# Attention masks of a two-layer graph network: 32x32 squares on VectorE, rows in blocks of 32, and left sides kept in SBUF

## The chip, the cores and the metric

The kernel runs on one core of one Trainium2 chip. The metric is the device time of one execution in microseconds (us). The median over six runs stands for the kernel, and one execution was recorded by the hardware profiler.

## The reference

There are N = 2708 nodes with D = 1024 features, all in fp32, and one integer adjacency matrix `adj` of 2708 x 2708. Both layers normalize, attend over the neighbours and add the result to their input. Biases and vectors are left out here where they change nothing in the shape of the work.

```
h  = relu(layernorm(x))
f  = h @ Wf + bf ;  g = h @ Wg + bg
e  = relu(f @ g.T)
x  = x + softmax(where(adj > 0, e, NEG)) @ (h @ W + bW)

h  = relu(layernorm(x)) @ W1
e  = leaky_relu(h @ a1 + (h @ a2).T, 0.2)
x  = x + relu(softmax(where(adj > 0, e, NEG)) @ h)
```

The mask of `adj` enters both layers. In the first layer it is added to the scores `e`; in the second it comes back from a copy in DRAM.

## The kernel before

**Tiling.** The 2708 rows are cut into five panels: `width` is 576, 576, 532, 512 and 512 rows, and `base` holds their starts. Each panel has F = 4 full tiles of 128 rows. The 64, 64 and 20 rows that are left over in the first three panels form two more tiles, `MONO` and `TINY`. `start_of_tile` (L95) and `places` (L97) say which rows of the input belong to which partitions of a tile; in this kernel a full tile is 128 rows in sequence. The twenty full tiles go in ten `pairs`, numbered q = 0 to 9, and the two left-over tiles are one more unit, `LEFT`. Nearly every large matrix product is made by a Strassen-Winograd scheme with seven half-sized products, M1 to M7.

**Stages of layer 0.** Wf and Wg are first multiplied into one matrix. Then each panel p goes through five steps. One multiplies the panel's rows by that matrix, `scores(p)` makes the scores against all rows, a softmax follows, one step aggregates, and `project` multiplies by W and adds the residual. The scores lie transposed: the panel's 512 to 576 rows run along the free axis, and the other nodes lie on the partitions. So the mask needs `adj` transposed as well. Layer 1 comes after the five panels.

**The loop of `scores(p)` (L1030).** For each pair q it forms seven products in the order M1, (M4 of the pair before), M6, M5, M2, M7, M3. `product` (L1043) loads the left sides `As` from `hs_d` in DRAM, two products at a time, and issues eight or four matmuls (L1052). VectorE takes each product out of PSUM with an addition; all VectorE instructions are issued through one helper, so they have line 45. `finish` then adds the mask, keeps the running maximum in `acc`, and, where layer 1's vectors are known, also updates the maximum for layer 1. While `nc.hold` is set, VectorE's instructions stay in program order. DMAs from SP go through `load` (L136) and always stay in program order; stores go from POOL (L140).

**The mask (`mask_maker`, L651).** `fetch(q)` loads a block of `adj` with SP, two pairs ahead. `convert(q)` turns it into 0 or minus BIG in bf16 (`nm`, and `nmt` for the 64 or 20 rows beyond 512). `turn(q)` transposes `nm` on TensorE in 128x128 blocks into a PSUM bank `mk_ps` (L700, tail L705), ScalarE copies the bank to `mask` (L701, L706), and POOL stores it to `mk_d` for layer 1. In the loop, `convert(q + 1)` stands behind M5's eviction and `turn(q + 1)` behind M3's. The first unit's three steps are done in the stages before (`first_masks`).

**Pairs in the background (`make_pairs`, L320).** Panel 0 finds its left sides being made as it goes. For each pair: x is loaded by SP, VectorE and ScalarE normalize, POOL forms sums for the aggregation (`pair_h`, L297), TensorE transposes (`h_ps`, L340), ScalarE copies to four tiles `hsT`, VectorE makes four sums in them, and POOL stores them to `hs_d`. `dots` form a bias per row. These steps are queued with `put`, each with an estimated cost, and `behind(rate)` takes some of them after each product, as much as a credit allows; `make_until(q)` forces the queue until pair q is made. In `scores` the two are called as

```
        rate = (0.6, 1.0, 0.65, 0.65, 0.65)[p]
            make_until(q + 2)
```

**Pools.** `slots` has 54 buffers, `strm` 12 (x blocks, `hsT`, `As`, `adj_i`, `g1` and `g2` share it) and `psum` 8 banks.

Of the kernel before, what the change touches and what calls it, by code (L numbers as in the profile page):

```python
# [10 lines left out]
I32 = mybir.dt.int32  # L11
# [46 lines left out]
def kernel(  # L58
# [22 lines left out]
    NH = NC // 2  # L81


    NP = N // W
    NM = P // 2
    NY = N - NP * W - P
# [5 lines left out]
    NT = TINY + 1  # L92
    full = lambda p: range(F * p, F * (p + 1))
    panel_of = [p for p in range(NP) for _ in range(F)] + [1, 2]
    start_of_tile = lambda t: base[t // F] + t % F * P  # L95

    places = [[(slice(0, P), start_of_tile(t))] for t in range(MONO)]  # L97
    places.append([(slice(0, NM), base[0] + W), (slice(NM, P), base[1] + W)])
    places.append([(slice(B32 * g, B32 * g + NY), base[2] + W) for g in range(P // B32)])

# [62 lines left out]

    ident = consts.tile([P, P], FP, name="ident")
    make_identity(nc, ident)
    identb = consts.tile([P, P], BF, name="identb")
    nc.vector.tensor_copy(identb, ident)
# [17 lines left out]
    def put(us, go, fetch=None, takes_psum=False, ready=None):  # L185
        later.append([us, fetch, go, takes_psum, ready])
# [128 lines left out]
    c0 = consts.tile([P, 1], FP, name="c0")  # L315
    r_ = consts.tile([P, NCOL], FP, name="r")
    vb = [None, None]
    made, turned_tiles = set(), set()

    def make_pairs():  # L320
        xs, hT = {}, {}
# [39 lines left out]
        def sums(q):  # L361
            if q == LEFT:
                return
            ts, i = hT.pop(q)
            at = {m: i(k) for k, m in enumerate(BY_SCORES)}
            add(at[M5], i(7), at[M4])
            sub(at[M6], at[M5], at[M1])
            sub(at[M7], at[M1], i(7))
            sub(at[M3], at[M2], at[M6])
            for g, t in enumerate(ts):  # L370
                store(hs_d[q][:, 2 * g:2 * g + 2].rearrange("p m c j -> p (m c j)"), t.rearrange("p m c j -> p (m c j)"))
# [28 lines left out]
        for i, q in enumerate(todo):  # L400
            if i + 1 < len(todo):
                put_norms(todo[i + 1])
            put_rows(q)
            put(0.5, lambda q=q: transposes(q), takes_psum=True)
            if i > 1:
                put_dots(q)
            put(2.7 if q != LEFT else 0.0, lambda q=q: last(q))
            if i == 1:
                put_dots(todo[0])
                put_dots(todo[1])  # L410
# [240 lines left out]
    def mask_maker(p):  # L651

        r0, w = base[p], width[p]
        k4 = w // P
        tail = w - k4 * P
        raw, neg = {}, {}

        def fetch(q):
            a = stream("adj_i", (P, k4, 2, P), I32)
            b = slot("adj_t", (P, 2, P), I32) if tail else None  # L660
            raw[q] = a, b
            body = adj[r0:r0 + k4 * P].rearrange("(i p) j -> p i j", p=P)
            last = adj[r0 + k4 * P:r0 + w]
            if q < LEFT:
                j0 = start_of_tile(pairs[q][0])
                load(a.rearrange("p i k j -> p i (k j)"), body[:, :, j0:j0 + 2 * P])
                if tail:
                    load(b[:tail].rearrange("p k j -> p (k j)"), last[:, j0:j0 + 2 * P])
                return
            for k, at, j, n in ((0, 0, base[0] + W, NM), (0, NM, base[1] + W, NM), (1, 0, base[2] + W, NY)):  # L670
                load(a[:, :, k, at:at + n], body[:, :, j:j + n])
                if tail:
                    load(b[:tail, k, at:at + n], last[:, j:j + n])

        def negate(o, i):
            nc.vector.tensor_scalar(o, i, 0.0, -BIG, op0=OP.is_le, op1=OP.mult)

        def convert(q):
            a, b = raw.pop(q)
            m = [slot("nm", (P, k4, 2, P), BF)]  # L680
            if tail:
                m.append(slot("nmt", (P, 1, 2, P), BF))
            for n, o, i in [(P, m[0], a)] + ([(tail, m[1], b.rearrange("p (o k) j -> p o k j", o=1))] if tail else []):
                if q < LEFT:
                    negate(o[:n], i[:n])
                    continue
                r = o.shape[1]
                nc.gpsimd.memset(o[:, :, 1], -BIG)
                negate(o[:n, :, 0], i[:n, :, 0])
                negate(o[:n, :, 1].rearrange("p i (g c) -> p i g c", c=B32)[:, :, :, :NY],  # L690
                       i[:n, :, 1:2, :NY].to_broadcast([n, r, P // B32, NY]))
            neg[q] = m

        def turn(q):
            m = neg.pop(q)
            mk = slot("mask", (P, 2, WX), BF)
            ps = bank("mk_ps", (P, 2, W), BF)
            for k in range(2):
                for i in range(k4):
                    nc.tensor.transpose(ps[:, k, i * P:(i + 1) * P], m[0][:, i, k], identb)  # L700
            nc.scalar.copy(mk[:, :, :k4 * P], ps[:, :, :k4 * P])  # L701
            if tail:
                ps = bank("mk_ps", (P, 2, W), BF)
                for k in range(2):
                    nc.tensor.transpose(ps[:, k, :tail], m[1][:tail, 0, k], identb[:tail, :tail])  # L705
                nc.scalar.copy(mk[:, :, k4 * P:w], ps[:, :, :tail])  # L706
            store(mk_d[p][:, q], mk[:, :, :w])
            mk_sb[p, q] = mk

        return fetch, convert, turn  # L710

# [2 lines left out]
    def first_masks(p, step):  # L714
        fetch, convert, turn = makers[p]
        if step == 0:
            fetch(0)
            fetch(1)
        elif step == 1:
            convert(0)  # L720
        else:
            turn(0)

    def load_mask(p, q, k):
        mt = slot("maskl", (P, WX), BF)
# [304 lines left out]
    def scores(p, B):  # L1030
# [6 lines left out]
        spread(rb, columns_of(p, r_[:, first_col[p]:]))  # L1037
        acc = slot("acc")
        S = [None] * NT
        rate = (0.6, 1.0, 0.65, 0.65, 0.65)[p]  # L1040
        lefts = {}

        def product(q, m, ps, start):  # L1043
            n, i = P, BY_SCORES.index(m)
            if i % 2 == 0:
                t = stream("As", (P, 2, NH, P))
                lefts[q] = t
                k = min(2, 7 - i)
                load(t[:, :k].rearrange("p m c j -> p (m c j)"),
                     hs_d[q][:, i:i + k].rearrange("p m c j -> p (m c j)"))  # L1050
            for c in range(NH):
                nc.tensor.matmul(ps[:n, :h], lefts[q][:, i % 2, c, :n], B[m][c // 2][:, c % 2, :h],  # L1052
                                 start=(start and c == 0), stop=(c == NH - 1), skip_group_check=True)
# [12 lines left out]
        def last(q, sb, Z, m1):  # L1066

            n = P
            product(q, M4, Z, False)
            add(sb[:n, lo], Z[:n, :h], m1[:n, lo])  # L1070
            finish(q, sb, 1)
            mk_sb.pop((p, q))
            behind(rate, True)

        nc.hold = True
        left_over = None
        for q in range(NQ):
            n = P
            make_until(q + 2)
            if q + 2 <= LEFT:  # L1080
                fetch(q + 2)
            sa, sb = slot("Sa"), slot("Sb")
            S[pairs[q][0]], S[pairs[q][1]] = sa, sb
            X, Y, Z = (bank(f"s{k}") for k in "xyz")
            m1, t = slot("sm1"), slot("st")
            product(q, M1, X, True)
            for s in (lo, hi):
# [12 lines left out]
            add(sa[:n, lo], X[:n, :h], rb[:n, lo])  # L1100
            behind(rate, True)
            product(q, M7, Z, False)
            add(sb[:n, hi], Z[:n, :h], t[:n, hi])
            behind(rate, True)
            product(q, M3, Y, False)
            add(sa[:n, hi], Y[:n, :h], t[:n, lo])
            finish(q, sa, 0)
            if q + 1 <= LEFT:
                turn(q + 1)
            behind(2 * rate, True)  # L1110
            left_over = lambda q=q, sb=sb, Z=Z, m1=m1: last(q, sb, Z, m1)

# [357 lines left out]
```

## Time and profile before

| what | value |
|---|---|
| median of six runs | 3165.61 us (3162.37 to 3167.58) |
| profiled execution | 3166.1 us, its span 3164.2 us |
| mean TensorE clock granted | 0.992 |
| layer 0 up to the second layer's products | 0 to 2182 us |
| of these, scores of panels 0 to 4 | 203-389, 660-810.5, 1073-1219, 1460-1600.4, 1780-1919.4 us |
| mask transposes on TensorE | 440 of 128x128, 66 for the tails |
| mask copies on ScalarE | 55 of 1011 ns, 33 for the tails |
| adjacency on VectorE, 128x1024 int32 | 50 of 704 ns on average |
| DMA traffic of the whole kernel | 650.47 MB, 206 GB/s on average |

The profile counts an engine as busy while it executes an instruction; waiting and the issue of DMAs do not count. A wait is written with the engine that waits, an arrow, and what released it. PE is TensorE, PEld its weight loads, DVE VectorE, ACT ScalarE, POOL GpSimd and SP SyncE. A stage ends when its last engine ends, so for each stage the reader has to ask which engine is the last there.

### The profile page before, as it was taken

To read this page: it belongs to the slowest core of one execution; us is meant where nothing else is said; L and a number is where in the kernel's file an instruction comes from. 1 tells how busy PE (TensorE), PEld (TensorE's weight loads), DVE (VectorE), ACT (ScalarE), POOL (GpSimd) and SP (SyncE) were. 2 spreads that over 40 slices of the span, in tenths; PEclk is the share of its full clock that TensorE was granted. 3 is DMA by queue.
4 is the path that set the end of the run, shared out by engine and by line. 5 is a ranking of instruction groups with operands and counts; after the bars stand their busy time and mean duration, and the time that the engine had idled before them with its cause. 6 is when DMAs were issued, how large, how long until landed. Compare 5 with 4: busy or idle time off the path is not lost.

```text
span 3164.2 us, 36134 instructions
## 1 busy us (share of the span) xinstructions
PE 3088.1 (98%) x13218; PEld 2292.1 (72%) x13218; DVE 1768.5 (56%) x3561; ACT 505.3 (16%) x872; POOL 411.8 (13%) x552
## 2 busy tenths in 40 slices
PE   8999999999999999999999999997999999999998
PEld 5576777667876688876888885864767758678684
DVE  7758576375722666327771357657574471744612
ACT  3412020010200112001020002203131130211200
POOL 3624102210002100023000101020010000100000
PEclk9999999999999999999999999998999999999999
DMA  7858749676446675467844567596555464555645
GB/s 272 317 195 293 263 140 346 193 250 213 142 130 190 212 250 179 140 196 240 276 153 152 172 206 223 197 299 214 200 174 180 152 204 153 171 195 176 212 156 195
DMA packets 273497, 650.47 MB, mean 206 GB/s; under 512 B 38160, under 2 KB 105720, under 8 KB 273320
## 3 DMA queue, kind: packets, MB, share of 16 engines
q1 hardware_dynamic: 232296, 524.04, 50.9%
q0 software_dynamic: 41024, 124.12, 11.3%
q8 instruction: 105, 1.72, 0.2%
q14 instruction: 72, 0.59, 0.1%
HBM read 535.37 MB, written 112.67 MB: 205 GB/s over the span
## 4 chain that ended last, share of the span: by engine, by line
PE 87%; issue 6%; DVE 3%; DMA 1%; POOL 1%; ACT 0%; SPq 0%; POOLq 0%; DVEq 0%; ACTq 0%
PE gy L545 11%; PE gz L545 11%; PE gx L545 11%; PE sz L1052 7%; PE pz L948 5%; PE sy L1052 5%; PE sx L1052 5%; PE gv L545 5%; PE px L948 3%; PE M_ps L465 3%; PE qz L545 3%; PE py L948 3%; PE qy L545 2%; PE qx L545 2%; PE po L921 1%
## 5 line engine op out<-in xcount | busy, mean ns | idle before, releaser
L1052 PE MATMUL sz<-B,As 128*128 128x288 f32 (+2 forms) x1200 | 295.8, 396 | 3.2 <-DVE st L45 3.2
L1052 PEld LDWEIGHTS sz<-B,As 128*128 128x128 f32 x1200 | 229.7, 192 | 50.8 <-DVE st L45 4.2
L856 POOL TENSOR_TENSOR gT<-gT,rr 128x2304 f32<-128x2304 f32 (+5 forms) x20 | 75.4, 3770 | 1088.5 <-DVE rr L45 1003.2
L1052 PE MATMUL sy<-B,As 128*128 128x288 f32 (+2 forms) x800 | 202.5, 397 | 4.6 <-DVE st L45 4.6
L1052 PE MATMUL sx<-B,As 128*128 128x288 f32 (+2 forms) x800 | 203.1, 397 | 3.4 <-DMA As<-hs_d 3.4
L545 PE MATMUL gz<-P,hc 128*128 128x288 f32 (+2 forms) x800 | 186.0, 393 | 2.3 <-ACT gT L845 2.3
L545 PE MATMUL gz<-Sa,hc 128*128 128x288 f32 (+2 forms) x800 | 186.0, 393 | 2.3 <-ACT gT L845 2.3
L545 PE MATMUL gx<-P,hc 128*128 128x288 f32 (+2 forms) x800 | 185.6, 394 | 0.0
L545 PE MATMUL gy<-T,hc 128*128 128x288 f32 (+2 forms) x800 | 184.2, 391 | 0.0
L1052 PEld LDWEIGHTS sy<-B,As 128*128 128x128 f32 x800 | 153.7, 192 | 36.7 <-DVE st L45 5.5
L545 PEld LDWEIGHTS gz<-Sa,hc 128*128 128x128 f32 x800 | 151.2, 190 | 36.0 <-ACT gT L845 4.4
L545 PEld LDWEIGHTS gz<-P,hc 128*128 128x128 f32 x800 | 150.9, 190 | 35.6 <-ACT gT L845 4.4
L545 PEld LDWEIGHTS gx<-P,hc 128*128 128x128 f32 x800 | 152.8, 191 | 32.6 <-issue 1.9
L545 PEld LDWEIGHTS gy<-T,hc 128*128 128x128 f32 x800 | 152.0, 190 | 30.5
L1052 PEld LDWEIGHTS sx<-B,As 128*128 128x128 f32 x800 | 149.1, 190 | 32.4 <-issue 3.9
L701 ACT COPY mask<-mk_ps 128x1024 bf16<-128x1024 bf16 x55 | 55.6, 1011 | 628.2 <-PE mk_ps L700 324.3
L948 PE MATMUL px<-w,gT 128*128 128x512 f32 x320 | 144.3, 603 | 6.3 <-issue 5.8
L948 PE MATMUL py<-w,ps 128*128 128x512 f32 x320 | 143.6, 598 | 0.0
L948 PE MATMUL pz<-w,ps 128*128 128x512 f32 x320 | 141.8, 593 | 0.0
L948 PEld LDWEIGHTS px<-w,gT 128*128 128x128 f32 x320 | 60.6, 193 | 82.9 <-issue 80.1
L45 DVE TENSOR_TENSOR gT<-gy,u 128x288 f32<-128x288 f32 (+2 forms) x40 | 14.8, 433 | 183.5 <-PE gy L815 183.5
L948 PEld LDWEIGHTS py<-w,ps 128*128 128x128 f32 x320 | 60.9, 192 | 76.2 <-issue 73.0
(326 smaller groups left out, 5070.2 us busy)
## 6 DMA issues: line engine op xcount, KB each, us to landing
hc<-hg_d SPq DMA_DIRECT2D x350, 512.0 KB
As<-hs_d SPq DMA_DIRECT2D x150, 512.0 KB
w<-wt_d SPq DMA_DIRECT2D x96, 512.0 KB
w<-in_L_gnn_W_dram SPq DMA_DIRECT2D x72, 512.0 KB
md<-md_d SPq DMA_DIRECT2D x56, 512.0 KB
adj_i<-in_adj_dram SPq DMA_DIRECT2D x50, 512.0 KB
hg_d<-g POOLq DMA_DIRECT2D x40, 512.0 KB, 4.9
hs_d<-hsT POOLq DMA_DIRECT2D x40, 512.0 KB, 5.3
```

Source lines behind the costliest of these rows:

```text
L45: i = f(*a, **k)
L465: nc.tensor.matmul(ps, wfT[a][c // NH][:, c % NH, :], wgT[b][c], start=(c == 0), stop=(c == NC - 1))
L545: nc.tensor.matmul(ps[d], left(m, k, d), right(m, k), start=(start and k == 0), stop=(k == K - 1 and m not in more), skip_group_check=True)
L701: nc.scalar.copy(mk[:, :, :k4 * P], ps[:, :, :k4 * P])
L856: nc.gpsimd.tensor_tensor(of(e, s), of(e, s), by(s, k), OP.mult)
L921: nc.tensor.matmul(ps, carry[:, e, k], w_[k], start=(start and k == 0), stop=(k == NH - 1), skip_group_check=True)
L948: nc.tensor.matmul(ps, left[i][m][:, k, :], w_[k], start=(start and k == 0), stop=(k == NH - 1), skip_group_check=True)
L1052: nc.tensor.matmul(ps[:n, :h], lefts[q][:, i % 2, c, :n], B[m][c // 2][:, c % 2, :h], start=(start and c == 0), stop=(c == NH - 1), skip_g ...
```

## The change

There are three edits.

1. A full tile no longer holds 128 rows in sequence. Tile t of a panel takes 32 rows out of each 128 of its 512: row 128 g + 32 s + r of the panel is on partition 32 g + r of tile s. Loads of x, of the residual, and stores of the output move 32 rows each, four times as many DMAs.
2. The adjacency block is fetched as four DMAs (and four more for a tail) of 32 partitions, with 64 columns in sequence. VectorE transposes it in 32x32 squares straight from `nm` to `mask`. TensorE's transposes, ScalarE's copies and the PSUM bank `mk_ps` are gone. The turn is split in two: its first half stands behind M2's eviction and its second behind M7's.
3. In panel 0, pairs that are made while the scores run keep their `hsT` tiles as left sides (`fresh`), and their `As` loads are gone. `make_until` is called with q + 1, the transposes of a pair wait until pair q - 1 is current, and the background rate is 1.7 until all pairs are made.

Instructions counted in the two programs: SP's DMAs 1364 and 1851, POOL's instructions 550 and 662, VectorE's 3363 and 3530 (110 transposes of 128x512, 66 for the tails); the 506 TensorE transposes and the 88 ScalarE copies of the mask are gone. Of the left sides, 135 loads of 512 KB remain of 150, and 45 of 256 KB remain of 50: five pairs of the ten are `fresh`.

```diff
-    start_of_tile = lambda t: base[t // F] + t % F * P
-    places = [[(slice(0, P), start_of_tile(t))] for t in range(MONO)]
+    start_of_tile = lambda t: base[t // F] + t % F * B32
+    places = [[(slice(B32 * g, B32 * (g + 1)), start_of_tile(t) + P * g) for g in range(P // B32)] for t in range(MONO)]
...
+    in_scores, now = [False], [0]
+    fresh = {}
...
             ts, i = hT.pop(q)
+            if in_scores[0]:
+                fresh[q] = ts
...
-            put(0.5, lambda q=q: transposes(q), takes_psum=True)
+            put(0.5, lambda q=q: transposes(q), takes_psum=True,
+                ready=lambda q=q: not in_scores[0] or q == LEFT or q <= now[0] + 1)
...
         def fetch(q):
-            a = stream("adj_i", (P, k4, 2, P), I32)
...
+            a = stream("adj_i", (P, NB, 2, B32), I32)
+            b = slot("adj_t", (P, tail, 2, B32), I32) if tail else None
             raw[q] = a, b
...
+            def square_rows(t, blocks, g, k, r, j, n):
+                load(t[B32 * g:B32 * (g + 1), :, k] if k is not None else
+                     t[B32 * g:B32 * (g + 1)].rearrange("p b k c -> p b (k c)"),
+                     adj[r:r + blocks * B32, j:j + n].rearrange("(b r) j -> r b j", r=B32))
+            for t, blocks, r in ((a, NB, r0), (b, tail, r0 + W)):
+                for g in range(NG if t is not None else 0):
+                    if q < LEFT:
+                        square_rows(t, blocks, g, None, r, c0[g], 2 * B32)
...
         def convert(q):
...
+                    m = slot("nm", (P, 2, blocks, B32), BF)
+                    nc.vector.tensor_scalar(m, t.rearrange("p b k c -> p k b c"), 0.0, -BIG, op0=OP.is_le, op1=OP.mult)
...
-        def turn(q):
...
-                    nc.tensor.transpose(ps[:, k, i * P:(i + 1) * P], m[0][:, i, k], identb)
-            nc.scalar.copy(mk[:, :, :k4 * P], ps[:, :, :k4 * P])
...
+        def turn(q, k):
+            if k == 0:
+                mk_sb[p, q] = slot("mask", (P, 2, WX), BF)
+            mk = mk_sb[p, q]
+            m = neg[q]
+            nc.vector.transpose(mk[:, k, :W].rearrange("p (s g r) -> p g s r", s=F, g=NG),
+                                m[0][:, k].rearrange("p (g s) c -> p g s c", g=NG))
             if tail:
...
+                nc.vector.transpose(mk[:, k, W:W + tail * B32].rearrange("p (b r) -> p b r", r=B32), m[1][:, k])
+            if k == 1:
+                neg.pop(q)
+                store(mk_d[p][:, q], mk[:, :, :w])
...
         def product(q, m, ps, start):
             n, i = P, BY_SCORES.index(m)
-            if i % 2 == 0:
+            if q in fresh:
+                lefts[q] = fresh[q][i // 2]
+            elif i % 2 == 0:
...
         for q in range(NQ):
-            n = P
-            make_until(q + 2)
+            n, now[0] = P, q
+            make_until(q + 1)
+            rate = 1.7 if NQ - 1 not in made else rates[p]
...
             add(sa[:n, lo], X[:n, :h], rb[:n, lo])
+            if q + 1 <= LEFT:
+                turn(q + 1, 0)
             behind(rate, True)
             product(q, M7, Z, False)
             add(sb[:n, hi], Z[:n, :h], t[:n, hi])
+            if q + 1 <= LEFT:
+                turn(q + 1, 1)
...
             finish(q, sa, 0)
-            if q + 1 <= LEFT:
-                turn(q + 1)
```

More of the change, by code (lines that the diff above doesn't have):

```diff
@@ L165 @@
     make_identity(nc, ident)
-    identb = consts.tile([P, P], BF, name="identb")
-    nc.vector.tensor_copy(identb, ident)
     eps = consts.tile([P, 1], FP, name="eps")
@@ L653, in mask_maker, with columns @@
         r0, w = base[p], width[p]
-        k4 = w // P
-        tail = w - k4 * P
+        NG, NB = P // B32, W // B32
+        tail = -(-(w - W) // B32)
         raw, neg = {}, {}
+        def columns(q):
+            if q < LEFT:
+                return [[start_of_tile(t) + P * g for g in range(NG)] for t in pairs[q]]
+            return [[base[g // 2] + W + g % 2 * B32 for g in range(NG)], [base[2] + W] * NG]
         def fetch(q):
-            a = stream("adj_i", (P, k4, 2, P), I32)
-            b = slot("adj_t", (P, 2, P), I32) if tail else None
+            a = stream("adj_i", (P, NB, 2, B32), I32)
+            b = slot("adj_t", (P, tail, 2, B32), I32) if tail else None
@@ L661, in fetch @@
             raw[q] = a, b
[L662 to L673, printed above, removed]
@@ L675, in negate @@
-        def negate(o, i):
-            nc.vector.tensor_scalar(o, i, 0.0, -BIG, op0=OP.is_le, op1=OP.mult)
+            c0, c1 = columns(q)
+            def square_rows(t, blocks, g, k, r, j, n):
[4 more added lines that the diff above has]
+                for g in range(NG if t is not None else 0):
+                    if q < LEFT:
+                        square_rows(t, blocks, g, None, r, c0[g], 2 * B32)
+                    else:
+                        for k, c in enumerate((c0, c1)):
+                            square_rows(t, blocks, g, k, r, c[g], B32)
@@ L678, in convert @@
         def convert(q):
             a, b = raw.pop(q)
-            m = [slot("nm", (P, k4, 2, P), BF)]
-            if tail:
[L682 to L691, printed above, removed]
@@ L692, in convert @@
-            neg[q] = m
-        def turn(q):
[L695 to L700, printed above, removed]
-            nc.scalar.copy(mk[:, :, :k4 * P], ps[:, :, :k4 * P])
[L702 to L708, printed above, removed]
+            neg[q] = []
@@ new lines, in convert @@
+            for t, blocks in ((a, NB), (b, tail)):
+                if t is not None:
+                    m = slot("nm", (P, 2, blocks, B32), BF)
+                    nc.vector.tensor_scalar(m, t.rearrange("p b k c -> p k b c"), 0.0, -BIG, op0=OP.is_le, op1=OP.mult)
+                    neg[q].append(m)
+        def turn(q, k):
[5 more added lines that the diff above has]
+                                m[0][:, k].rearrange("p (g s) c -> p g s c", g=NG))
+            if tail:
+                nc.vector.transpose(mk[:, k, W:W + tail * B32].rearrange("p (b r) -> p b r", r=B32), m[1][:, k])
+            if k == 1:
+                neg.pop(q)
+                store(mk_d[p][:, q], mk[:, :, :w])
@@ L721, in first_masks @@
         else:
-            turn(0)
+            turn(0, 0)
+            turn(0, 1)
     def load_mask(p, q, k):
@@ L1039, in scores @@
         S = [None] * NT
-        rate = (0.6, 1.0, 0.65, 0.65, 0.65)[p]
+        rates = (0.6, 1.0, 0.65, 0.65, 0.65)
         lefts = {}
@@ L1072, in last @@
             mk_sb.pop((p, q))
+            fresh.pop(q, None)
             behind(rate, True)
-        nc.hold = True
+        nc.hold = in_scores[0] = True
         left_over = None
         for q in range(NQ):
-            n = P
-            make_until(q + 2)
+            n, now[0] = P, q
+            make_until(q + 1)
+            rate = 1.7 if NQ - 1 not in made else rates[p]
             if q + 2 <= LEFT:
```

## Prediction

> **What bounds the kernel now.** I read the page's busy shares and its chain first, then how much room the other engines have in each scores stage.
>
> ```profile
> PE 3088.1 (98%) x13218; PEld 2292.1 (72%) x13218; DVE 1768.5 (56%) x3561; ACT 505.3 (16%) x872; POOL 411.8 (13%) x552
> PEclk9999999999999999999999999998999999999999
> PE 87%; issue 6%; DVE 3%; DMA 1%; POOL 1%; ACT 0%; SPq 0%; POOLq 0%; DVEq 0%; ACTq 0%
> ```
>
> TensorE is busy for 98% of the span and carries 87% of the chain. Work that leaves TensorE shortens the span, unless what replaces it makes TensorE wait. The mask's turn is such work. The groups of the tile `mk_ps`, the waits of TensorE, and TensorE's timeline around one turn in the first and one in the last panel:
>
> ```profile
> L700 PE MATMUL mk_ps<-identb,nm x440: 219/219/230, 194.3 to 1907.5; 128*128 128x128 bf16 x147
> L705 PE MATMUL mk_ps<-identb,nmt x66: 166/190/237, 194.9 to 1206.7; 64*128 64x64 bf16 x44, 20*128 20x20 bf16 x22
> ...
> PE mk_ps L700 <- DVE nm L45: 9.6, 7, 3.8
> PE sy L1052 <- DVE st L45: 4.6, 2, 2.6
> PE sx L1052 <- DMA As<-hs_d: 3.4, 1, 3.4
> PE sz L1052 <- DVE st L45: 3.2, 2, 2.9
> ```
>
> ```profile
> 280.92 0.61 PE L700 MATMUL mk_ps<-identb,nm 128*128 128x128 bf16 x8
> 281.47 0.23 PE L705 MATMUL mk_ps<-identb,nmt 64*128 64x64 bf16 x2
> 281.63 1.97 PE L340 MATMUL h_ps<-ident,x 128*128 128x128 f32 x16
> ...
> 1844.20 0.61 PE L700 MATMUL mk_ps<-identb,nm 128*128 128x128 bf16 x8
> 1844.65 1.95 PE L1052 MATMUL sx<-B,As 128*128 128x256 f32 x8
> 1846.43 3.62 PE L1052 MATMUL sz<-B,As 128*128 128x256 f32 x16
> ```
>
> Matmuls overlap, so a group's price is the distance to the next start, not its duration: 281.63 - 280.92 = 0.71 us in the first panel, where a tail is turned too; 0.45 us in the last, and the product behind it takes 1.78 us where its neighbours take 1.73, so 0.50. The stages of the scores, panels 0 to 4 (columns: window, its length, busy us and instructions of PE, PEld, DVE, ACT, POOL; clock, DMA share, GB/s), then single pairs: one with new pairs made in panel 0, one full and one light of the later panels:
>
> ```profile
> 203.00:389.00 186.00, 172.57 (x815) 132.44 (x814) 128.34 (x249) 32.87 (x60) 49.15 (x65) 0.96 0.78 273
> 660.00:810.50 150.50, 146.72 (x682) 112.95 (x681) 83.00 (x166) 12.84 (x22) 10.51 (x19) 0.99 0.68 224
> 1073.00:1219.00 146.00, 145.58 (x737) 120.45 (x736) 96.82 (x209) 15.26 (x28) 14.16 (x22) 1.00 0.74 242
> 1460.00:1600.40 140.40, 137.11 (x714) 118.42 (x713) 104.42 (x218) 15.02 (x19) 18.87 (x32) 1.00 0.80 263
> 1780.00:1919.40 139.40, 139.40 (x733) 120.98 (x732) 77.70 (x153) 10.49 (x11) 14.86 (x19) 1.00 0.67 210
> ...
> 280.60:304.50 23.90, 18.35 (x84) 13.76 (x83) 20.20 (x38) 6.66 (x12) 11.15 (x14) 0.93 0.84 295
> 710.60:725.00 14.40, 14.40 (x70) 11.21 (x68) 7.32 (x15) 1.18 (x2) 0.54 (x1) 1.00 0.59 190
> 1485.70:1498.40 12.70, 12.70 (x67) 11.14 (x66) 11.15 (x28) 2.71 (x4) 2.15 (x4) 1.00 0.73 218
> 1853.00:1865.60 12.60, 12.60 (x66) 11.06 (x65) 7.82 (x15) 1.01 (x1) 0.73 (x1) 1.00 0.63 190
> ```
>
> VectorE has some 5 to 7 us free in a light pair, 1 to 2 in a full one, and little in the pairs of panel 0 that also make new pairs, where TensorE already waits.
>
> **1. The turn leaves TensorE: gain.** Five panels of eleven turns. Panels 0 and 1: 11 x 0.70 = 7.7 us each. Panel 2 (tail of 20 rows, 0.68): 7.5. Panels 3 and 4 (no tail): 5.5 each. Sum 33.9. With it goes the wait for `nm`, 9.6 us: 3.78 in panel 1, 2.19 in panel 0, 3.3 in panel 3, 0.34 in panel 2. It does not all come back. In panel 1 VectorE ran behind (dots back to back from 670 to 675), and its late `st` evictions would have held the next product about a us later, so I credit 2.8 there. ScalarE's copies (55 of 1.01 us, 33 of at most 0.27) and POOL's eight memsets go too, but neither engine bounds a stage: nothing for them.
>
> **2. The turn arrives on VectorE: cost.** The changed kernel has 110 transposes of 128x512 bf16 and 66 tails. The trace holds no VectorE transpose. Its nearest rows move 512 elements per partition in 0.68 to 0.74 us (`nm`, with 1,024 int32, also takes 0.68); bounds are half of that (0.34, if bf16 were taken two at a time) and 2 us (three times the row, for an operation that works square by square and writes with a stride). I take 0.68, and 0.15 for a tail (the smallest rows). That is 1.66 us more per pair in panels 0 to 2 and 1.36 in 3 and 4, in all 110 x 0.68 + 66 x 0.15 = 85 us on VectorE. A light pair hides it: 7.32 + 1.66 = 9.0 of 13.7, 7.82 + 1.36 = 9.2 of 12.1. Each transpose is in VectorE's fixed order directly behind an eviction; what queues behind it is background work and then M3's or M4's eviction, and TensorE waits only when that comes later than the bank's next product. In a full pair the room is gone. Panel 3: 11.15 + 1.36 = 12.5 against a shortened 12.2; seven such pairs lose some 0.5 us each, 3.5. Panel 2: two pairs at 12.0 + 1.6 against 12.7: 2. Panel 1: three at about 11.5 + 1.7 against 13.7: up to 1. Panel 4: none.
>
> The Trainium skill, "VectorE: DVE Perf Modes", section "The three transpose paths", gives 390 ns for a 128x128 bf16 block on TensorE and 311 ns on VectorE, which there turns only 32x32 squares, and its "Rules for kernel authors" sends a 128x128 transpose to TensorE. The trace shows eight TensorE blocks passing in 0.45 to 0.55 us. By the page's price a 512-wide transpose would be an estimated 4 x 0.311 = 1.24 us, and the forecast would be nearly all eaten: some 20 us more lost in the full pairs.
>
> `nm`'s input is now read in runs of 32 elements; I keep its 0.68 us. If it were twice that, the same eighteen full pairs would pay 0.7 us each, 12 us.
>
> **3. Masks come in 8 (or 4) DMAs instead of 2 (or 1), with runs of 256 bytes instead of 1 KB.** The trace's packets on that queue take 19.5 ns at 256 bytes and 53.7 ns at 1,024; spread over 16 engines a body rises from 512 x 53.7 / 16 = 1.7 to 2,048 x 19.5 / 16 = 2.5 us. SP issues for 0.38 to 0.5 us each: 3.2 us per pair instead of 0.9. A pair lasts 12.6 us or more, SP carries some 15 to 20 short issues then, and the fetch is two pairs ahead: nothing, if that cover holds. If it goes, `convert` waits on VectorE with evictions behind it, at a us or two per pair.
>
> The Trainium skill, "DMA: Bandwidth & Descriptors", asks for at least 512 bytes per descriptor and for batching, which speaks against this; at a DMA share of 0.67 to 0.80 I read it as a cost in reserve, not in time.
>
> **4. Rows 32 at a time.** Loads of x and of the residual go from 80 to 320 issues, stores of the output from 40 to 160. In the project stages 24 more SP issues x 0.36 plus the first masks' are 14 to 17 us, but the next weights lie 20 us or more ahead of their use: nothing. At the start, `wf` loads that sit behind 12 more x issues would land about 2 us later than their 17.98 and 19.27 us; they are needed at 24.65: nothing. POOL's 120 more issues of 0.54 us (65 us) lie beside TensorE work except the last: that store was issued at 3156.81, and the end came at 3164.2. Three more issues are +1.6 us, quicker landing of smaller pieces gives some back (3.3 us for 128 KB, 4.7 for 256): +1.2, between +0.5 and +1.8.
>
> **5. Panel 0.** Its excess over bare products is about 22 us, and 13.4 of that is named in the waits (10 on VectorE, 3.43 on `As`). Pairs 5 to 9 now use `hsT` from SBUF: 20 `As` loads go, and their wait. But these pairs are made in fewer scores pairs. The listing puts norms, dots and sums of three pairs together: base 6.9, the turn 1.7, dots 3.2, sums 2.5, norms 4.5, and some 4.2 of VectorE operations stretched beside POOL's `pair_h`, so 23 us, and with a wait 24 to 24.5. My pairs: 3 x 13.6 + 15.4 + 24 + 24.5 + 24.5 + 17 + 2 x 13.6 + 13 = 186, against 183 now: what the turn and `As` save, the crowding costs. I take 0, with -15 (the stalls go with their loads) to +12 (x comes late: sixteen x issues and eight masks' on SP, and a stream ring of twelve buffers that eight `hsT`, two `g` and two `adj_i` fill).
>
> **Sum.** Panel 0: 0. Panel 1: -7.7 - 2.8 + 1.0 = -9.5. Panel 2: -7.5 - 0.3 + 2.0 = -5.8. Panel 3: -5.5 - 3.3 + 3.5 and 0.5 for the narrower cover = -4.8. Panel 4: -5.5. Tail: +1.2. Together -24.4. The profiled execution took 3166.1 us (span 3164.2); the median is 3165.61, 0.5 lower. So 3166.1 - 24.4 - 0.5 = 3141 us.
>
> **The rivals.**
> - *VectorE becomes the bound in the full pairs* (slower). At 2 us a transpose, a pair needs 4.3 us: three pairs of panel 1 lose 2.3 each, six of panel 2 2.8, seven of panel 3 3.2, three of panel 0 2.6 beyond what part 5 holds; 54 us against 39 won (33.9 + 2.8 + 0.3 + 3.3 - 0.5 - 1.2), so +15 us, 3181. It decides from about 1.6 us per transpose, where the same sum gives 39. For it: no transpose in the trace, the strided output. Against: every other VectorE row of 512 elements is at 0.68 to 0.74.
> - *Panel 0 crowds* (small gain to none). At +12 there and twice the losses of part 2: -24.4 + 12 + 6.5 = -6, 3160. For it: VectorE at 20.2 of 23.9 us and the denser making. Against: the pairs' total VectorE work is unchanged but for the turn.
> - *The stalls of panel 0 go as well*: -20 there, 3121. For it: 3.43 us of `As`, 2.19 of `nm`, 0.9 of the clock in the slow pairs. Against: most waits there are for VectorE.
> - *The edit does little of what it says.* Half holds: pairs 0 to 4 still go through DRAM. It is in the sum.
>
> **How the numbers follow.** The forecast's case (-38 to -12, 3128 to 3154): 0.45. The larger gain: 0.15. Gain mostly eaten: 0.19, of which 0.07 falls within 0.2% (6.3 us, what a measurement of this kernel can tell from no change). VectorE or panel 0 worse than that: 0.21. Faster 0.72, same 0.07, slower 0.21. For 8 in 10 I cut some 0.06 of the largest gains and 0.14 of the worst cases: 3116 to 3172.
>
> **What would show it.** Right: no `mk_ps`, VectorE transposes near 0.68 us, panel 4's pairs at 12.1 us, panel 1 at about 141, TensorE's `L1052` waits for `st` under 10 us outside panel 0. Wrong: transposes at 1.4 us or more, `nm` waiting for `adj_i`, or panel 0 over 198 us.

## The result, and the profile after

The changed kernel takes 3177.04 us (median of 16 runs, 3170.43 to 3179.7) against 3166.01 us of the kernel before (36 runs): a ratio of 1.0034, 95% interval 1.0027 to 1.004. It is slower by some 11 us, where the prediction said 25 us faster. The profiled execution's span is 3173.6 us against 3164.2, 9.4 us longer.

The page of the changed kernel, its engines and its chain:

```profile
PE 3057.2 (96%) x12712; PEld 2265.4 (71%) x12712; DVE 1834.1 (58%) x3728; ACT 444.0 (14%) x783; POOL 463.8 (15%) x664
PE 88%; DVE 5%; DMA 3%; issue 2%; POOL 1%; SPq 1%; ACT 0%; DVEq 0%; POOLq 0%; ACTq 0%
```

TensorE does 31 us less work, and the span is longer all the same: it now waits about 40 us more. The waits of TensorE in the changed kernel (total in us, number, longest), and VectorE's transposes as groups (count, busy us, mean ns):

```profile
PE sz L1053 <- ACT hsT L359: 26.3, 2, 13.2
PE pz L947 <- DVE x_res L45: 8.2, 3, 5.6
PE wT_ps L457 <- DVE wgT L45: 7.7, 1, 7.7
PE px L947 <- DVE pt L45: 5.0, 1, 5.0
...
L45 DVE STREAM_TRANSPOSE mask<-nm 128x512 bf16<-128x512 bf16 x110 | 76.9, 700 | 0.0
L45 DVE STREAM_TRANSPOSE mask<-nm 128x64 bf16<-128x64 bf16 x44 | 9.0, 204 | 0.0
```

Two waits of 13 us for `hsT` are new; the wait for `pt` has grown from 0.5 us, those for `x_res` from 2.6 and the one for `wgT` from 4.7. The waits for `nm` and `As` are gone. A transpose costs 0.70 us. The scores stages, panels 0 to 4, in the columns used above:

```profile
207.40:410.50 203.10, 164.17 (x709) 126.22 (x710) 139.73 (x287) 22.09 (x40) 47.99 (x63) 0.91 0.62 200
671.40:821.80 150.40, 147.86 (x629) 113.86 (x630) 104.87 (x227) 3.28 (x7) 11.91 (x21) 1.00 0.81 235
1085.10:1223.90 138.80, 136.65 (x630) 113.93 (x630) 108.52 (x247) 4.19 (x8) 13.47 (x20) 1.00 0.85 253
1465.10:1602.70 137.60, 132.32 (x631) 113.65 (x629) 114.80 (x237) 4.82 (x8) 17.37 (x28) 1.00 0.92 270
1785.40:1916.10 130.70, 130.70 (x630) 114.12 (x629) 89.25 (x172) 0.37 (x1) 14.87 (x19) 1.00 0.74 209
```

TensorE is idle for 39 us of panel 0, at a granted clock of 0.91; panel 4 has no gap at all. To compare kernels I cut every run in the same way: a stage lasts from its first matmul to the first matmul of the next kind of stage (so the turn of each panel's first mask falls into a stage before its scores). What differs, in us; every stage left out, among them all of layer 1 up to the last projection, is equal within 0.1 except those named below the table:

| stage (start in the kernel before) | before | after | rows by 32 alone | all but edit 3 | edit 3 alone |
|---|---|---|---|---|---|
| start, weights (4) | 143.4 | +4.7 | +3.6 | +4.5 | +0.6 |
| scores, panel 0 (204) | 185.3 | +17.8 | -1.3 | +4.5 | +15.3 |
| scores, panel 1 (650) | 160.6 | -10.2 | +1.1 | -10.2 | +0.1 |
| scores, panel 2 (1075) | 144.4 | -5.6 | 0 | -5.6 | 0 |
| scores, panel 3 (1461) | 139.7 | -2.1 | 0 | -2.0 | 0 |
| scores, panel 4 (1783) | 135.7 | -5.0 | 0 | -5.0 | 0 |
| projection (1919) | 54.3 | +4.1 | +3.6 | +4.9 | 0 |
| projection (2107) | 76.0 | +7.6 | +7.2 | +5.6 | 0 |

The first masks' turns save another 3.4 us in five other stages; the first aggregation (445) costs 0.7, the tail 0.8.

### The profile page after: what moved, and what is told of

The parts are those of the page before. It is cut to its first block, busy times and chain, and to the rows that moved or that the text cites. A ratio compares the mean times of both kernels' runs of the same rounds, so it can differ in the third digit from the quotient of the medians.

```text
span 3173.6 us, 36179 instructions
## 1 busy us (share of the span) xinstructions
PE 3057.2 (96%) x12712; PEld 2265.4 (71%) x12712; DVE 1834.1 (58%) x3728; ACT 444.0 (14%) x783; POOL 463.8 (15%) x664
## 4 chain that ended last, share of the span: by engine, by line
PE 88%; DVE 5%; DMA 3%; issue 2%; POOL 1%; SPq 1%; ACT 0%; DVEq 0%; POOLq 0%; ACTq 0%
PE gz L549 12%; PE gy L549 11%; PE gx L549 11%; PE sz L1053 7%; PE pz L947 6%; PE gv L549 6%; PE px L947 4%; PE sy L1053 4%; PE py L947 4%; PE sx L1053 4%; PE M_ps L469 3%; PE qz L549 3%; PE qy L549 2%; PE qx L549 2%; PE po L920 1%
## 5 line engine op out<-in xcount | busy, mean ns | idle before, releaser
L1053 PE MATMUL sz<-B,As 128*128 128x256 f32 (+2 forms) x1080 | 263.4, 393 | 16.2 <-DVE st L45 15.5
L1053 PEld LDWEIGHTS sz<-B,As 128*128 128x128 f32 x1080 | 205.4, 191 | 59.9 <-DVE st L45 19.6
L1053 PE MATMUL sx<-B,As 128*128 128x256 f32 (+2 forms) x720 | 178.4, 391 | 1.4 <-DVE sm L45 1.4
L1053 PE MATMUL sy<-B,As 128*128 128x256 f32 (+2 forms) x720 | 179.0, 392 | 0.0
L1053 PEld LDWEIGHTS sy<-B,As 128*128 128x128 f32 x720 | 137.5, 191 | 27.1 <-DVE st L45 0.3
L1053 PEld LDWEIGHTS sx<-B,As 128*128 128x128 f32 x720 | 136.2, 190 | 28.1 <-DVE sm L45 2.2
L143 POOL DMA_DIRECT2D out_dram<-x_res x180 | 88.9, 501 | 266.3 <-DVE x_res L45 230.4
L143 POOL DMA_DIRECT2D mk_d<-mask x55 | 35.9, 653 | 570.6 <-DVE mask L45 531.9
```

The source lines that it names most:

```text
L143: nc.gpsimd.dma_start(a, b)
```

## The experiments

**The three edits apart.** Four runs; the last three columns above are three of them. First without edit 3:

```diff
-            if in_scores[0]:
-                fresh[q] = ts
-                ready=lambda q=q: not in_scores[0] or q == LEFT or q <= now[0] + 1)
-            make_until(q + 1)
-            rate = 1.7 if NQ - 1 not in made else rates[p]
+            make_until(q + 2)
+            rate = rates[p]
```

> Edits 1 and 2 stay; edit 3 is undone: left sides from DRAM for all pairs, make_until(q + 2), the old rate, no gate on the transposes. Theory A (edit 3 costs panel 0 its 17.8 us through the stream ring): the scores stage of panel 0 falls from 203.1 us to 185.3 - 7.7 = 178 or a little more, no wait of TensorE for hsT is left, and the whole is 3177 - 25 = about 3152 us. Rival B (VectorE's transposes fill the crowded pairs of panel 0): that stage stays at 195 us or more, and the whole at 3168 or more.

Measured: 3161.42 us, ratio 0.9984 (0.9976 to 0.9993). Panel 0 falls from 203.1 to 189.7 us, so edit 3 costs 13.4 there; but the stage ends between the two forecasts, with a new wait of TensorE in it: 17.5 us for `As` (this run, all of it in panel 0):

```profile
PE sx L1050 <- DMA As<-hs_d: 17.5, 4, 8.7
```

Next, the kernel before with its row traffic cut and nothing else:

```diff
-    places = [[(slice(0, P), start_of_tile(t))] for t in range(MONO)]
+    places = [[(slice(B32 * g, B32 * (g + 1)), start_of_tile(t) + B32 * g) for g in range(P // B32)] for t in range(MONO)]
```

> The kernel before, with only its row traffic cut: every full tile is loaded and stored in four DMAs of 32 rows, rows still in sequence. Theory A (the number of row DMAs costs the start of the kernel 4.7 us, the project stage at 1919 us 4.1 and the one at 2106 us 7.6): all three appear here, and the whole is about 3166 + 16 = 3182 us. Rival C (those stages moved because the instruction orders changed with the mask): the three stages stay within 1 us of before, and the whole is 3166 plus 1 to 3 us.

Measured: 3179.82 us, ratio 1.0039 (1.0025 to 1.0052). The three losses appear at 3.6, 3.6 and 7.2 us: the number of row DMAs alone explains 14.4 of the 16.4 us that the start and the two projections lose. How it does is seen on SP's queue before the last projection, first of the kernel before (its stage starts at 2106.57), then of this run (2114.37), with TensorE's answer:

```profile
2086.56 0.80 SPq L138 DMA_DIRECT2D x_res<-in_x_dram  x2
2087.62 6.64 SPq L138 DMA_DIRECT2D w<-wt_d  x4
```

```profile
2102.41 7.68 SPq L138 DMA_DIRECT2D x_res<-in_x_dram  x8
2110.41 2.20 SPq L138 DMA_DIRECT2D w<-wt_d  x4
...
2114.37 3.70 PE L948 MATMUL px<-w,gT 128*128 128x512 f32 x8
2123.05 6.51 PE L948 MATMUL px<-w,gT 128*128 128x512 f32 x8 [4.98 <-DVE pt L45]
```

In the kernel before, `x_res` takes eight issues here and 3.3 us of SP's queue in all; in this run 32 issues and 19.3 us. The weights of the stage were asked for 19 us ahead of it, and now 4 us ahead; such a load lands 5.1 us after its issue (median in the changed kernel). TensorE's order has changed with it: `py`, which needs those weights, no longer stands between the two `px`, so the second `px` waits for VectorE, and its eight matmuls then take 6.5 us instead of 3.7.

Edit 3 alone on the kernel before (the diff of the change's edit 3, nothing else):

> The kernel before with edit 3 alone: fresh left sides and the new pace, the turn on TensorE, rows and masks loaded as before. Theory A: two or three waits of TensorE for hsT of 10 us or more, the scores stage of panel 0 at 185.3 + 17.8 + 7.7 = about 210 us, the whole at about 3190 us. Rival B: without VectorE's transposes the crowded pairs have room, the stage stays at 180 to 190 us, and the whole within 5 us of 3166.

Measured: 3183.55 us, ratio 1.0052 (1.0039 to 1.0064). Panel 0 is at 200.6 us: the cost, 15.3 us, is there without VectorE's transposes, so rival B falls. But the stage stays under the 210 us of theory A, and TensorE waits 25.1 us for `st`, not for `hsT`: my theory named the wrong wait for this kernel.

The permuted rows in one DMA instead of four:

```diff
-                load(o[e][ps], a[r:r + ps.stop - ps.start, e * W:(e + 1) * W])
+                load(o[e], a[b0:b0 + W, e * W:(e + 1) * W].rearrange("(g s r) d -> s g r d", g=P // B32, s=F)[t % F])
```

> As the run without edit 3, but the permuted rows of a full tile move in one DMA whose DRAM side walks four blocks of 32 rows, instead of four DMAs. Theory A: the 16 us of the row DMAs go, so about 3152 - 16 = 3136 us. Rival C (order, not number of DMAs): about the same as the run without edit 3, within 3 us.

Measured: 3218.49 us, ratio 1.0158 (1.0144 to 1.0172), worse than four. The start grows by 15.7 us, the next stage by 20.8 (a wait of 19.3 for ScalarE's `m`), the last projection by 10.6. In the first 30 us SP's issues of x took up to 5.8 us each here, 0.33 to 0.65 in the kernel before. Why such a load is slow was not tried further.

**What holds panel 0.** In the changed kernel the copies to `hsT` on ScalarE wait 34.9 us for `hg_d<-g`, POOL's store of a pair's sums: both live in the ring `strm` of twelve buffers. One such round, VectorE, POOL, ScalarE and TensorE:

```profile
321.61 4.04 DVE L45 SCALAR_TENSOR_TENSOR Sb<-Sb,mask 128x576 f32<-128x576 f32 x1
325.68 1.70 DVE L45 TENSOR_TENSOR acc<-acc,Sb 128x576 f32<-128x576 f32 x1
...
320.77 0.53 POOL L143 DMA_DIRECT2D hs_d<-hsT  x1 [0.67 <-DVE hsT L45]
321.32 1.27 POOL L302 TENSOR_TENSOR g<-x 128x512 f32<-128x512 f32 x1
326.71 1.48 POOL L143 DMA_DIRECT2D hg_d<-g  x2
...
330.07 0.59 ACT L359 COPY hsT<-h_ps 128x512 f32<-128x512 f32 x1 [14.80 <-DMA hg_d<-g]
...
330.71 3.74 PE L1053 MATMUL sz<-B,hsT 128*128 128x288 f32 x8 [13.18 <-ACT hsT L359]
```

POOL's four sums stand behind the last `hs_d` store of the pair before, which waits for VectorE; they run from 321 us, just where VectorE adds a mask (4.04 us instead of 0.76) and updates `acc` (1.70 instead of 0.76); their stores are issued up to 328 us, and at 330 the copy to the next `hsT`, released by them, begins, and TensorE goes on. That the ring is what holds the sums back until then is inferred: x was normalized by 310 us, but the trace names no wait of the first sum.

Two things are at work, and the other runs show that they can come apart. ScalarE waits for `hg_d<-g` in the changed kernel alone, and in the run with thirteen buffers below. In the kernel before it is SP's queue that waits for these stores, since its loads use the same ring (its waits in panel 0):

```profile
SPq L138 <- DMA hg_d<-g: 35.7, 7, 11.9
```

With edit 3 alone SP waits so for 23.6 us. Common to all three kernels are the stretched mask adds: three in panel 0, each 3.4 to 4.1 us beside POOL's sums. So I moved the sums to the pool `slots`:

```diff
-        g1, g2 = stream("g1", (P, 2, W)), stream("g2", (P, 2, W))
-        s1, s2, s3, s4 = g1[:n, 0], g1[:n, 1], g2[:n, 0], g2[:n, 1]
+        s1, s2, s3, s4 = (slot(f"g{k}")[:, :W] for k in range(4))
...
+        for m, s in zip(range(M5, M3 + 1), (s1, s2, s3, s4)):
+            store(hg_d[l][i][:n, m, j], s)
```

> The changed kernel with the four sums that POOL makes for a pair (g1, g2) in buffers of the slots pool, so that they no longer share the ring of twelve with hsT, As and adj_i. Theory A (the ring: hsT waits until POOL's sums are stored): the two 13 us waits of TensorE for hsT go and the scores stage of panel 0 falls from 203 to about 183 us, the whole to about 3157. Rival D (VectorE: the run with edit 3 alone waited 25 us for st, not for hsT): the waits come back as waits for st of some 7 us each, the stage stays at 197 to 201, the whole at 3171 to 3175.

Measured: 3145.45 us, ratio 0.9933 (0.9918 to 0.9949). Panel 0 falls by 25.7 us to 177.3, further than theory A said, and the last projection by 9.9. The start and the stage ahead of panel 0 grow by 1.4 and 6.4 (a wait of 4.5 us for `qT`), so these two and panel 0 together fall by 18.0. The long waits are gone, and of the mask adds one is left that is stretched, to 2.14 us (stage and waits of this run):

```profile
214.90:392.20 177.30, 163.49 (x711) 125.59 (x710) 132.83 (x286) 21.80 (x40) 51.93 (x71) 0.96 0.71 230
...
PE sz L1052 <- DVE st L45: 12.0, 11, 3.3
PE sz L1052 <- DVE hsT L45: 8.7, 3, 4.8
```

Two more runs of the same question. The changed kernel with left sides from DRAM but the new pace (the two `fresh` lines of the first diff alone taken out):

> The changed kernel with the left sides of all pairs loaded from DRAM again; the pace (make_until(q + 1), the gate, rate 1.7) stays. Theory A (hsT tiles held by their pair block the ring): the stage of panel 0 falls to 185 to 190 us. Rival D (the pace crowds VectorE, whatever the tiles): it stays at 197 us or more, and may be longer, since As of a pair just stored has to come back from DRAM.

Measured: 3174.3 us, 1.0023 (1.0014 to 1.0032); panel 0 at 202.9 us, with 27.1 us of waits for `st` and 8.0 for `As`, as rival D said. So holding the tiles is not the cause: the new pace is. Four mask adds take 4.05 us here, and it is SP's queue that waits for `hg_d<-g`, 47.0 us; no copy to `hsT` does. And the ring one buffer longer (`strm` 13, `slots` 53):

> The changed kernel with one more buffer in the stream ring (13, slots 53), the sums still in it. Theory A (the ring's length): the waits for hsT fall clearly below the 26 us of the changed kernel, and panel 0 to 180 to 195 us. Rival I (it is the moment of POOL's sums, beside VectorE's work, and one buffer does not move it): panel 0 stays at 200 or more.

Measured: 3171.28 us, 1.0014 (1.0005 to 1.0024); panel 0 at 201.9, waits for `hsT` on ScalarE's copy down to 19.0, others up, and three mask adds still at 4.0 to 4.1 us. One buffer does not help; that the sums leave the ring does. Whether the blocked buffer or the moment of POOL's sums weighs more was not separated: moving them cures both. That the stage is as long with the pace alone, where no copy to `hsT` is blocked, speaks for more than the block.

**Was the ring tight before?** The kernel before, with that move alone:

> The kernel before with only POOL's (and in layer 1 VectorE's) sums moved to the slots pool: the control for the mended runs. If the ring held back the old kernel too (its panel 0 waited 10 us for VectorE), its scores stage of panel 0 falls from 185 to about 175 and the stage at 2106 us from 76 to 68 as in the run with the mended edit 3, whole about 3148; edit 3, mended, would then be a loss of 5 us. If the ring was tight only with edit 3, panel 0 stays at 185 and only the later stages move, whole about 3155.

Measured: 3146.65 us, 0.9935 (0.9923 to 0.9948), 20 us faster than before without any part of the change. Panel 0 is at 176.4 us, panel 1 5.2 shorter (its wait of 3.8 us for `nm` is gone), the last projection 7.7 shorter. The whole change with the same move (3145.45 us, 0.9918 to 0.9949) cannot be told from it. The same move beside edit 3 alone:

> The kernel before with edit 3 alone (the run that took 3184 us), and POOL's sums in the slots pool. Theory A (the ring, and with it the moment of POOL's sums, is all that is wrong with edit 3): the scores stage of panel 0 falls from 200.6 to about 177.4 + 7.7 = 185 us, so the whole to about 3168, and the waits for st from 25 to some 12 us. Rival D (VectorE is crowded without the ring): the stage stays at 195 or more, the whole at 3177 or more.

Measured: 3153.26 us, 0.9959 (0.9947 to 0.9972); panel 0 at 185.3, with 13.9 us of waits for `st` left in it. And beside edits 1 and 2 alone:

> Edits 1 and 2 without edit 3, and the sums out of the ring. If edit 3, once mended, is worth something, panel 0 stays above the 177.4 us of the mended changed kernel, at 183 to 190, since As is still awaited (17.5 us without the mending); if edit 3 is worth nothing, panel 0 falls to 177 or below.

Measured: 3152.01 us, 0.9958 (0.9946 to 0.9971); panel 0 at 181.0, just under the first forecast, with 15.3 us of waits for `As`. So with the ring mended, edit 3 costs 8.9 us of panel 0 in the old kernel (185.3 against 176.4), and saves 3.7 beside edits 1 and 2 (177.3 against 181.0), where `As` is late. It pays only against a loss that its two companions bring. The move does not cure all of it: in the old kernel edit 3 cost 15.3 us of panel 0 with the sums in the ring, and costs 8.9 without; the waits for `st` are left.

**Rows in sequence.** Edit 2 without the permutation: one row DMA again, but adjacency runs of 128 bytes in eight to sixteen DMAs. This kernel leaves out the matching order of the mask's columns, so the masks are added at other places; all instructions have the same sizes.

```diff
-                        square_rows(t, blocks, g, None, r, c0[g], 2 * B32)
+                        square_rows(t, blocks, g, k, r, c[g], B32)
```

> Edit 2 alone: VectorE's turn, but tiles keep 128 rows in sequence and move in one DMA; the two tiles of a pair then lie 128 columns apart, so the adjacency comes in eight (with a tail sixteen) DMAs of 128-byte runs. Edits 1 and 3 are gone. Theory: the 26 us won by the turn in panels 0 to 4 stay, the 15.6 us of the row DMAs go (start 143.4, stage at 1919 us 54.3 or less, stage at 2106 us 76.0), and As waits in panel 0 shrink because x takes four issues: 3166 - 26 + 0 to 4 = 3140 to 3145 us. Rival E (the adjacency's small runs are what delays As in panel 0): the waits for As stay at 15 us or grow, panel 0 stays at 190 or more, the whole at 3146 to 3155.

Measured: 3178.85 us, 1.0035 (1.0022 to 1.0049). The projections lose nothing (52.8 and 76.3 us), but `As` is awaited 44.4 us in twelve places: panel 0 at 195.1, panel 1 at 163.1, panel 2 at 153.4. Rival E, and worse. The permuted rows were there for a reason: they give 256-byte runs in half as many DMAs. Which of the two weighs more was not separated.

**Rows from other queues**, on top of the mended changed kernel. ScalarE issues the residual's rows:

```diff
-                load_rows_of(t, xs[t], x)
+                load_rows_of(t, xs[t], x, nc.scalar)
```

> The run with POOL's sums out of the ring, and the 160 loads of the residual's rows issued by ScalarE instead of SP. Theory F (SP's queue: thirty-two row loads ahead of the stage's weights delay them, and the instructions behind are ordered around that): the stage at 1919 us falls from 58.5 to about 54 us, that at 2106 us from 73.7 to about 70, TensorE's 5 us wait for pt there goes; whole 3145 - 8 = 3137 us. Rival G (VectorE's order, not the queue): both stages stay within 1 us, whole 3145.

Measured: 3149.95 us, 0.9947 (0.9934 to 0.9959). The last projection falls to 67.3 us; the one at 1919 us rises to 69.2. ScalarE's own queue shows why:

```profile
1893.48 27.93 ACTq L256 DMA_DIRECT2D x_res<-in_x_dram  x32
1921.45 1.07 ACT L953 COPY pt<-px 128x512 f32<-128x512 f32 x2 [27.70 <-DMA x_res<-in_x_dram]
```

The issues hold ScalarE for 28 us, with an eviction behind them; TensorE waits 10.3 us for it. With the early rows of x on ScalarE too:

> As the run before, and the rows of x loaded ahead of the scores are issued by ScalarE too. Theory F: the first stage falls from 149.4 to about 143.5 us and the wait for qT in the second goes, whole 3137 - 8 = 3129 us. Rival H (ScalarE, held by the issues, delays its copies of the weights at the start): the first stage stays at 148 or grows.

Measured: 3169.85 us, 1.0012 (1.0003 to 1.0021); the start at 152.1 us, the stage behind it at 78.5 (20.9 us for `rs`). Only the last panel's rows on ScalarE, where it copies nothing:

> The run with POOL's sums out of the ring; of the residual's rows only those of the last panel (the stage at 2106 us) are issued by ScalarE, which copies nothing there while they are issued. Theory F (what is ahead of the stage's weights on the issuing queue decides): that stage at 67.3 us as with all rows from ScalarE, the one at 1919 us stays at 58.5, whole 3145 - 6.5 = 3139 us. Rival: the stage's gain came from the other rows and it stays at 73.7.

Measured: 3142.14 us, 0.9922 (0.991 to 0.9935): the best run, ahead of both kernels, with the last projection at 67.3 us as forecast; against the kernel before with the sums moved (0.9923 to 0.9948) its interval overlaps. Then the early x from POOL:

> As the run before, and the rows of x that are loaded ahead of the scores are issued by POOL, which does nothing from 3 to 22 us. Theory F (SP's queue at the start: sixteen x issues ahead of wf): the first two stages fall from 149.4 and 61.4 us to about 144 and 56, whole 3139 - 11 = 3128 us. Rival H (x itself comes late on any queue, and VectorE's order waits for it): the first stage stays at 148 or more.

Measured: 3172.82 us, 1.0018 (1.0009 to 1.0028); the start grows to 158.4 us and the next stage to 86.5. And, left on SP, the first sixteen x issues moved behind two more `wf` loads:

> The best run so far (3142 us), with the first pair's sixteen x issues moved behind the second two wf loads. If what stands ahead of wf on SP's queue makes the first stage longer, it falls from 150.6 to about 145 us and the whole to 3137. If it is VectorE's order (bn of x ahead of the copies of wgT, on x that comes late), the first stage stays at 150 or grows, since x comes later still.

Measured: 3145.26 us, 0.9935 (0.9922 to 0.9947); the start stays at 150.6, but the loss has moved. TensorE's wait for `wgT` falls from 8.4 us in the best run to 2.9, and its second group of `wf` transposes starts at 23.80 us instead of 30.18. Then the next `wf` is late, since it now stands behind 32 x issues (SP and TensorE of this run):

```profile
7.62 22.96 SPq L139 DMA_DIRECT2D x<-in_x_dram  x32
30.62 2.05 SPq L139 DMA_DIRECT2D wf<-in_L_gnn_Wf_dram  x4
37.14 3.60 PE L456 MATMUL wT_ps<-ident,wf 128*128 128x128 f32 x16 [4.56 <-DMA wf<-in_L_gnn_Wf_dram]
```

So the place of the x issues on SP's queue does matter to the start: early, they make the copies of `wgT` late, and further back, the next `wf`. VectorE's order is part of the first: in the changed kernel the statistics of x (16.15 us) stand ahead of the copies of `wgT` (17.60), here the copies come first (12.90, the statistics at 22.76). An order of SP's queue that spares both was not tried.

**Is VectorE's room priced rightly?** The best run with each 512-wide transpose issued twice:

```diff
+            for _ in range(2):
+                nc.vector.transpose(mk[:, k, :W]...
```

> The 3142 us run (sums out of the ring, last residual from ScalarE) with each 512-wide VectorE transpose issued twice: 1.4 us more per pair, 77 us more on VectorE. By the prediction's working (a light pair hides it, a full pair pays all of it) panel 4 stays at 130.7, panel 1 gains three pairs x 1.4 = 4 at most, panel 2 six x 1.4 = 8, panel 3 seven x 1.4 = 10 us: the stages at 154, 147 and 147 us, with panel 0 some 5 more, whole about 3142 + 25 = 3167. Rival: the full pairs still have room (TensorE's banks decouple them for longer than a pair), the later panels pay less than half of that, whole at 3155 or less.

Measured: 3166.39 us, 0.9998 (0.9988 to 1.0007), 24 us more than the best run. Panels 0 to 4 pay 3.7, 1.7, 7.0, 9.6 and 0.0 us, where 5, 4, 8, 10 and 0 were expected.

## Why the prediction was wrong

**Right: the turn (parts 1 and 2).** Panel 1 was forecast at -9.5 and came at -10.2, panel 2 at -5.8 and -5.6, panel 4 at -5.5 and -5.0; panel 3 at -4.8 and only -2.1: its DMA share rose to 0.92 and VectorE to 114.8 of 137.6 us, but which of them cost the rest was not tested. In panel 1 the agreement is partly luck: the moved sums alone bring 5.2 us there in the old kernel, and beside them the turn brings 5.0 (150.4 against 155.4), where the prediction had 7.7 - 1.0 without the wait for `nm`. The first masks' 3.4 us lie outside these stages. The transpose was taken at 0.68 us and measured 0.70, the tails at 0.15 and 0.17 to 0.20. The doubled run shows that a light pair hides it and a full pair pays for it, within about 1 us per stage in panels 2 to 4 and 2.3 in panel 1; the rival of VectorE as the bound did not come. By the price of the Trainium skill ("VectorE: DVE Perf Modes", section "The three transpose paths") it would have been an estimated 1.24 us; the trace decides for 0.70. The Trainium skill also names 512 bytes as the least transfer for line rate ("DMA: Bandwidth & Descriptors", section "Specifications"). The runs agree in one respect: runs of 128 bytes instead of 256, in twice as many DMAs, brought 44 us of waits for `As`; 256 bytes showed as 17.5 us of such waits in panel 0, together with the row DMAs. (The eighteen full pairs of the prediction's last sum in part 2 do not follow from its lists, which give 16 in panels 1 to 3.)

**Wrong: part 5, panel 0.** Forecast 0 with bounds of -15 and +12; measured +17.8. The step that failed is the sum of VectorE's work per pair, which was to come out even. It left out the ring as a link. I had written that `hsT`, the sums and `adj_i` fill twelve buffers, and used it only as a reason for late x. In the changed kernel the chain runs through it, from POOL's sums over their store to the next `hsT`, and their moment stretches VectorE's mask adds; taking the sums out gives 25.7 us there, 18.0 with the two stages ahead. By which of its two ways the ring costs more is open. I also put the old stage's 10 us of VectorE waits down to crowding, as a given: the control shows that 8.9 us of that stage went with the same move. (The sum set 186 us against 183 for the old stage, which by the cut above lasts 185.3. Its own sign of being wrong, panel 0 over 198 us, came.)

**Wrong: part 4, the row DMAs.** Forecast 0 and a tail of 1.2; measured 4.7, 4.1 and 7.6 us and a tail of 0.8. The step that failed is the cover, the lead of the weights that was to hide the issues. I took it as 20 us or more in every projection. In the last it was 19 us, and the rows took 16.0 us more of it than before: 32 issues at 0.60 us each in place of eight at 0.41, where 24 more at 0.36 had been assumed. So 4 us were left, and `py` no longer stood between the two `px`. At the start I followed when `wf` lands, and not what VectorE and ScalarE have queued behind x.

**Not foreseen in part 3:** eight adjacency DMAs beside sixteen of x make `As` late in panel 0 (17.5 us of `sx` waits when edit 3 does not take the loads away, 4.4 with the row DMAs alone). I had called it a cost in reserve; panel 0 is 5.7 us longer than with the row DMAs alone (189.7 against 184.0), although the turn has left TensorE there.

So 16.4 us in the stages of the row DMAs, 17.8 in panel 0 and 1.5 elsewhere (the first aggregation and the tail) stand against about 26 won, where 24 net were forecast.

## What to carry to other kernels

A ring of buffers that several engines share is an edge in the chain: list who must give a buffer back before who can start, before summing work per engine. A cover is checked in every stage in which the moved transfers are issued, and the thinnest one decides. Before crediting an edit with curing a stall, try the plainest cure of that stall in the old kernel: here moving four tiles gave 20 us, and beside that move edit 3 alone made the old kernel 6.6 us slower (3153.26 against 3146.65).

## What the runs showed of the hardware

Some of VectorE's operations are stretched beside POOL's elementwise sums: a masked add took 4.04 us instead of 0.76 at 321 us, and `acc` 1.70; with the sums moved to `slots` ten of the eleven adds to `Sb` took 0.76. Others were not: in that run additions out of PSUM stayed at 0.45 us and the transposes at 0.70 beside the same sums. A VectorE transpose of 128x512 bf16 in 32x32 squares took 0.70 us with a permuted output. With one DMA that walks four blocks of 32 rows in place of four DMAs, the kernel took 3218 us against 3161. Thirty-two DMA issues of 64 KB kept ScalarE's queue for 28 us.
